# A graph layer on one core: comparisons, casts and copies of VectorE in the edge blocks written as operations of two tensors

## The chip, the cores and the metric

The kernel runs on one core of a Trainium2 chip. The metric is the device time of one execution in microseconds (us); the time before is the median of three runs.

A core has five engines that work through instruction streams of their own: TensorE (PE in the profile; its weight loads are listed as PEld), VectorE (DVE), ScalarE (ACT), GpSimd (POOL) and SyncE (SP). They wait for each other through semaphores. SBUF is the on-chip memory of 128 partitions, PSUM the memory that TensorE's products land in.

## The reference

A graph with 12,500 nodes (64 features each) and 212,500 edges, which come sorted by `dst` while the sums go to `src`. With `h` the normalised nodes:

```
h   = relu(layernorm(x))
e   = silu([h[src], h[dst], weight] @ eW1 + eb1)
e   = silu(e @ eW2 + eb2)
agg = segment_sum(e, src, 12500)
out = x + silu([h, agg] @ nW1 + nb1) @ nW2 + nb2
```

The first product is split: `h[src] @ eW1[:64] + eb1` and `h[dst] @ eW1[64:128]` are made once for each node and then picked for each edge.

## The kernel before

**Prologue.** The nodes are normalised and the two products are written to tables in HBM, `tb` for destinations and later `ta` for sources, each number as a sum of three bf16 parts. The edges lie in 208 blocks of 1024. A source's id n is split into n % 100 (its bucket, one of `NB` = 100) and n // 100 (its place within the bucket, `locE`). Bucket numbers, and destinations relative to the block's first one, go to HBM as bf16 rows (`rows`).

**Stage one, for each block: sort the edges into buckets.** The 208 blocks form 11 chunks, the first of 8 blocks and the others of 20. For a block:

- `load` (L372) fetches, from SP's queue, the block's two bf16 rows broadcast to the partitions (`bc`), a window of 112 rows of `tb` (`win`), and three rows of the weights into the tail of `pick`.
- `count` (L389) runs on VectorE. L395 makes the one-hot matrix `pick` (112 x 1024, bf16): destination number equal to the partition's number. L397 makes `oh` (100 x 1024, fp16): bucket equal to the partition's number. L400 is a scan along the edges that counts how many edges of the bucket have come so far; it starts from `carry`, the count at the end of the block before. L406 copies the last count to a small fp32 tile `end`, which becomes `carry`. L408 multiplies counts by `oh`, so that each edge keeps only the count in its own bucket.
- `send` (L417) has TensorE sum the columns of that product (`rank`, L427), which gives each edge's rank in its bucket, and multiply `pick` by `win` (L435), which gives each edge its destination's row. ScalarE copies these rows to `qs` (L442). VectorE turns rank and bucket into row addresses `to` (L445) and writes the edge's place within its bucket into the last 16 columns of `qs` (L449). GpSimd then scatters 128 rows at a time to HBM by an indirect DMA (L454), 8 scatters a block, 1661 in all. There are 8 buffers `qs` of four scatters each, and 4 of `to`.

**Stage two, for each chunk: work off the buckets.** A chunk's rows in HBM are read in 25 batches of four buckets (`fetch`, L489), five batches ahead. A batch of a chunk can be fetched only when every scatter of the chunk has landed. For 512 edges, a step, the work is: TensorE spreads the places (`s_lr`, L515), VectorE compares them with the partition number (`s_one_t`, L526, from PSUM), TensorE adds the source's row (`s_pt`), ScalarE applies silu, TensorE multiplies by `eW2` (`s_p2`), ScalarE applies silu, VectorE makes a one-hot matrix of places (`s_one`, L553: both inputs in SBUF, fp32), TensorE sums by it (`s_seg`, L587), and after each batch VectorE adds to the totals (`s_add`, L598). The last chunk's batches also produce the output.

**The order.** PE, DVE, ACT and SP run in an order written out by hand: `turn` (L605) lists the parts of a step, and at each `None` in it the loop inserts pieces of stage one for the next chunk, paced so that a chunk's sends are issued shortly before its first batch is fetched. A piece of `count` and a piece of `send` for the block before go together. GpSimd has only the scatters in its queue.

Of the kernel before, what the change touches and what calls it, by code (L numbers as in the profile page):

```python
# [28 lines left out]
F32 = mybir.dt.float32  # L29
F16 = mybir.dt.float16  # L30
BF16 = mybir.dt.bfloat16
I32 = mybir.dt.int32
AF = mybir.ActivationFunctionType
OP = mybir.AluOpType
# [4 lines left out]
P = 128  # L39
L = 125  # L40
WL = 112
BLK = 1024
# [3 lines left out]
W = 144  # L46
# [11 lines left out]
def tile_gnn(ctx: ExitStack, tc: tile.TileContext, x, src, dst, ew, eW1, eb1, eW2, eb2, nW1, nb1, nW2, nb2, out):  # L58
    nc = tc.nc
    N, D = x.shape  # L60
    H = eW2.shape[0]
    E = src.shape[0]
    assert D == 64 and H == P and N % L == 0
    NB = N // L
# [6 lines left out]
    const = ctx.enter_context(tc.tile_pool(name="const", bufs=1))  # L71
# [12 lines left out]
    zeros = const.tile([P, 4 * W], F32, name="zeros")  # L84
# [54 lines left out]
    part = const.tile([P, 1], F32, name="part")  # L139
    nc.vector.tensor_copy(part, part_i)  # L140
    part1 = const.tile([P, 1], F32, name="part1")
    nc.vector.tensor_scalar(part1, part, 1.0, None, op0=OP.add)
    nodes_i = const.tile([P, L], I32, name="nodes_i")
    nc.gpsimd.iota(nodes_i, pattern=[[1, L]], base=1, channel_multiplier=0)
    nodes1 = const.tile([P, L], F32, name="nodes1")
# [50 lines left out]
    locE = const.tile([P, 2 * TB, NP], F32, name="locE")  # L196
# [4 lines left out]
    with tc.tile_pool(name="pro", bufs=1) as pro, tc.tile_pool(name="norm", bufs=2) as np_, tc.tile_pool(  # L201
        name="nab", bufs=2
# [154 lines left out]
    with tc.tile_pool(name="ld", bufs=4) as ld, tc.tile_pool(name="ld2", bufs=NQ) as ld2, tc.tile_pool(  # L357
        name="wk", bufs=2
    ) as wk, tc.tile_pool(name="qs", bufs=8) as qsp, tc.tile_pool(name="to", bufs=4) as top, tc.tile_pool(
        name="mm", bufs=4, space=PSUM  # L360
# [7 lines left out]
        blk = {}  # L368
# [20 lines left out]
        def count(s):  # L389

            if s >= nblocks:
                return
            c = chunk_of[s]
            bc, win, pick = blk[s]
            nc.vector.tensor_scalar(pick[:WL, :], bc[:WL, 0, :], part[:WL, :], None, op0=OP.is_equal)  # L395
            oh = wk.tile([NB, BLK], F16, name="oh")
            nc.vector.tensor_scalar(oh, bc[:NB, 1, :], part[:NB, :], None, op0=OP.is_equal)  # L397
            yield
            run = wk.tile([NB, BLK], F16, name="run")
            nc.vector.tensor_tensor_scan(  # L400
                run, oh, nil.to_broadcast([NB, BLK]), carry.get(c, 0.0), op0=OP.add, op1=OP.add
            )
            yield
            end = wk.tile([NB, 1], F32, name="end")
            n = min(BLK, E - s * BLK)
            nc.vector.tensor_copy(end, run[:, n - 1 : n])  # L406
            carry[c] = end
            nc.vector.tensor_tensor(run, run, oh, op=OP.mult)  # L408
            blk[s].append(run)
            if s + 1 == nblocks or chunk_of[s + 1] != c:  # L410
                u = wk.tile([NB, 1], F32, name="u")
                for limit, op in ((chunks[c][2] * P, OP.is_gt), (chunks[c][3], OP.is_lt)):
                    nc.vector.tensor_scalar(u, end, float(limit), None, op0=op)
                    nc.vector.tensor_tensor(bad[:NB, 1:2], bad[:NB, 1:2], u, op=OP.add)
            yield

        def send(s):  # L417

            p, g = s // 2, s % 2
            c = chunk_of[s]  # L420
            _, _, cap, _, q = chunks[c]
            _, win, pick, run = blk.pop(s)
            n = min(BLK, E - s * BLK)
            nt = -(-n // P)
            rank = misc[:, (s % 2) * TB : (s % 2 + 1) * TB]
            for t in range(nt):
                nc.tensor.matmul(rank[:, t : t + 1], run[:, t * P : (t + 1) * P], ones16[:NB, :], start=True, stop=True)  # L427
            yield
            for t0 in range(0, nt, G):
                qs = qsp.tile([P, G, W], F32, name="qs")  # L430
                qp = mm.tile([P, G, H], F32, name="qp", tag="mm")
                m = min(G, nt - t0)
                for t in range(m):
                    for i in range(3):
                        nc.tensor.matmul(  # L435
                            qp[:, t, :],
                            pick[: WL + 3, (t0 + t) * P : (t0 + t + 1) * P],
                            win[: WL + 3, i, :],
                            start=i == 0,
                            stop=i == 2,  # L440
                        )
                nc.scalar.copy(qs[:, :m, :H], qp[:, :m, :])  # L442
                if t0 == 0:
                    to = top.tile([P, TB], I32, name="to")
                    nc.vector.scalar_tensor_tensor(  # L445
                        to[:, :nt], rank[:, :nt], float(cap * P + 1), bkE[:, g * TB : g * TB + nt, p], op0=OP.min, op1=OP.add
                    )
                at = g * TB + t0
                nc.vector.tensor_copy(  # L449
                    qs[:, :m, H:], locE[:, at : at + m, p][:, :, None].to_broadcast([P, m, W - H])  # L450
                )
                for t in range(t0, t0 + m):
                    k = min(P, n - t * P)
                    i = nc.gpsimd.indirect_dma_start(  # L454
                        out=q[:],
                        out_offset=bass.IndirectOffsetOnAxis(ap=to[:k, t : t + 1], axis=0),
                        in_=qs[:k, t - t0, :],
                        in_offset=None,
                    )

                    tc.declare_no_dep(i.ins, group=f"rows{c}", reason="each edge has a row of its own")
                    tc.add_to_no_dep_group(f"rows{c}", i.ins)
                yield

        def send_all(c):

            mine = [s for s in range(nblocks) if chunk_of[s] == c]
            zeros_left = list(fill(c + 1, nc.scalar, 25)) if c + 1 < len(chunks) else []
            each = -(-len(zeros_left) // len(mine))
            for s in mine:  # L470
                load(s + 2, 1)
                for f in zeros_left[:each]:
                    f()
                del zeros_left[:each]

                for i, _ in enumerate(itertools.zip_longest(count(s + 1), send(s))):
                    pending[c] -= i == PIECES - 1
                    yield
# [159 lines left out]
        for _ in count(0):  # L638
            pass
# [17 lines left out]
        at = done = 0  # L657
# [25 lines left out]
    with tc.tile_pool(name="fl", bufs=1) as fl, tc.tile_pool(name="flp", bufs=1, space=PSUM) as flp:  # L683
        fp = flp.tile([1, P], F32, name="fp")
        s = fl.tile([P, 1], F32, name="s")
        nc.vector.tensor_tensor(s, bad[:, 0:1], bad[:, 1:2], op=OP.add)
        nc.tensor.transpose(fp, s, ident)
        m = fl.tile([1, 1], F32, name="m")
# [134 lines left out]
```

## Time and profile before

| | |
|---|---|
| Median of 3 runs | 2708.69 us (2707.8 to 2714.96) |
| Profiled execution, its own time | 2708.9 us |
| Its span | 2706.9 us |
| PE busy | 2321.1 us (86%) |
| VectorE busy | 1846.2 us (68%) |
| ScalarE busy | 1204.1 us (44%) |
| GpSimd (POOL) busy | 1723.0 us (64%) |
| Scatters L454 | 1661, mean 1030 ns, 1710.3 us |
| Mean granted clock of TensorE | 0.915 |

The span is the time between the first and the last instruction that the profile shows. A row of a group names line, engine, operation, output and inputs, shapes and count, then busy time in us, the mean of one in ns, and the idle time of the engine just ahead of these instructions, with what ended it. "issue" stands for a wait that nothing in the profile explains. A row of the timeline has start and duration in us and, in brackets, the engine's idle time before it and what ended it. The slices divide the span in 40 equal parts, one digit each, in tenths of busy time.

### The profile page before, as it was taken

Reading aid. Unit: us, or ns where it says so; the run is one execution under the profiler, and the core shown is the slowest. Engines: PE = TensorE matmul, PEld = TensorE weight load, DVE = VectorE, ACT = ScalarE, POOL = GpSimd, SP = SyncE. Lnnn points to the kernel's source line nnn. Section 1 sums busy time; section 2 is a strip of 40 time slices with the busy share of each in tenths; the row PEclk is TensorE's granted clock in tenths of the full one; section 3 lists DMA queues with packets and bytes.
Section 4 is the critical chain, followed back from the end, with each engine's and each line's share of the span. In section 5 each row is a group of like instructions: output and inputs, shape, how many; then the busy total and the mean of one; then the engine's idle time right before and its main releaser. Section 6 shows DMA issues by size and latency. Waiting matters only on the chain. (4 is left out here: it accounts for less than half of the span.)

```text
span 2706.9 us, 61144 instructions
## 1 busy us (share of the span) xinstructions
PE 2321.1 (86%) x23583; PEld 2168.2 (80%) x23583; DVE 1846.2 (68%) x3287; ACT 1204.1 (44%) x2247; POOL 1723.0 (64%) x1691
## 2 busy tenths in 40 slices
PE   1656688799799699799979979979979979979998
PEld 0445577799699699799879979979979979978886
DVE  5745468688588588678768768868858868743332
ACT  2522234355355355355445435535535545534442
POOL 1036577777777777777777777777777777750000
PEclk9755689899899899999989989989989989989998
DMA  6477867987787697697797787788688758644441
GB/s 180 170 210 208 246 226 227 284 276 231 237 280 244 211 288 247 200 312 245 214 293 254 224 274 252 246 247 269 229 248 272 244 185 267 216 173 127 137 128 33
DMA packets 388692, 612.85 MB, mean 226 GB/s; under 512 B 47232, under 2 KB 294401, under 8 KB 387877
## 3 DMA queue, kind: packets, MB, share of 16 engines
q1 hardware_dynamic: 269560, 423.47, 48.7%
q0 software_dynamic: 53760, 122.94, 13.3%
q10 hardware_dynamic: 65074, 62.46, 9.4%
q8 instruction: 188, 3.08, 0.5%
q14 instruction: 110, 0.90, 0.1%
HBM read 393.49 MB, written 215.18 MB: 225 GB/s over the span
## 5 line engine op out<-in xcount | busy, mean ns | idle before, releaser
L454 POOL DMA_INDIRECT q<-qs,to x1661 | 1710.3, 1030 | 679.2 <-issue 386.4
L546 ACT ACTIVATE e<-pt 128x512 f32<-128x512 f32 x525 | 313.7, 597 | 926.5 <-PE pt L542 765.1
L573 PE MATMUL p<-w,e 128*128 128x128 f32 x4200 | 578.7, 282 | 102.3 <-ACT p L567 102.3
L573 PEld LDWEIGHTS p<-w,e 128*128 128x128 f32 x4200 | 523.6, 196 | 117.1 <-ACT p L567 104.3
L526 DVE TENSOR_SCALAR oneT<-lr,part 125x512 bf16<-125x512 f32 x525 | 392.3, 747 | 325.8 <-PE lr L521 325.7
L587 PE MATMUL seg<-one,e 128*128 128x125 f32 x4200 | 581.2, 282 | 19.8 <-DVE aggT L598 14.6
L587 PEld LDWEIGHTS seg<-one,e 128*128 128x128 f32 x4200 | 523.6, 196 | 22.6 <-ACT qs L442 11.7
L400 DVE TENSOR_TENSOR_SCAN run<-oh,end,misc 100x1024 f16<-100x1024 f16 x197 | 461.1, 2340 | 6.4 <-PE misc L427 5.8
L542 PE MATMUL pt<-oneT,a 125*128 125x256 bf16 (+1 forms) x3300 | 440.1, 272 | 0.0
L435 PE MATMUL qp<-win,pick 115*128 115x128 bf16 x4983 | 369.1, 227 | 37.1 <-DVE oneT L526 30.4
L442 ACT COPY qs<-qp 128x512 f32<-128x512 f32 x416 | 243.3, 585 | 286.5 <-PE qp L435 218.3
L435 PEld LDWEIGHTS <-pick 115*128 115x128 bf16 x4983 | 330.4, 102 | 45.3 <-issue 40.8
L553 DVE TENSOR_TENSOR one<-nodes,qt 128x500 f32<-128x500 f32 x525 | 352.2, 671 | 0.7 <-PE seg L587 0.5
L542 PEld LDWEIGHTS <-a 125*128 125x128 bf16 x3300 | 317.8, 99 | 33.5
L535 PE MATMUL pt<-ident,qt 128*128 128x128 f32 x2100 | 329.5, 281 | 3.1 <-DVE prest L187 2.2
L577 ACT ACTIVATE e<-p 128x512 f32<-128x512 f32 x525 | 313.2, 597 | 12.9 <-PE p L573 9.6
L567 ACT COPY p<-b2f 128x512 f32<-128x512 f32 x525 | 311.8, 594 | 0.0
L598 DVE TENSOR_TENSOR aggT<-aggT,seg 128x500 f32<-128x500 f32 x250 | 168.2, 673 | 152.5 <-PE seg L587 152.3
L521 PE MATMUL lr<-identb,qt 128*125 128x128 bf16 x2100 | 210.6, 224 | 62.2 <-DMA qt<-q 62.2
L521 PEld LDWEIGHTS <-qt 128*125 128x125 bf16 x2100 | 187.2, 140 | 64.0 <-DMA qt<-q 63.3
L535 PEld LDWEIGHTS pt<-ident,qt 128*128 128x128 f32 x2100 | 227.6, 144 | 4.0 <-DVE prest L187 2.3
L408 DVE TENSOR_TENSOR run<-run,oh 100x1024 f16<-100x1024 f16 x208 | 144.3, 694 | 7.1
(118 smaller groups left out, 1264.4 us busy)
## 6 DMA issues: line engine op xcount, KB each, us to landing
qt<-q SPq DMA_DIRECT2D x250, 576.0 KB
a<-ta SPq DMA_DIRECT2D x275, 384.0 KB
bc<-rows SPq DMA_DIRECT2D x208, 448.0 KB
q<-zeros ACTq DMA_DIRECT2D x40, 1462.5 KB
q<-qs,to POOLq DMA_INDIRECT x1661
win<-tb SPq DMA_DIRECT2D x208, 84.0 KB
tb<-parts SPq DMA_DIRECT2D x25, 384.0 KB
ta<-parts SPq DMA_DIRECT2D x25, 384.0 KB
```

What stands on the lines that cost most here:

```text
L400: nc.vector.tensor_tensor_scan(run, oh, nil.to_broadcast([NB, BLK]), carry.get(c, 0.0), op0=OP.add, op1=OP.add)
L435: nc.tensor.matmul(qp[:, t, :], pick[: WL + 3, (t0 + t) * P : (t0 + t + 1) * P], win[: WL + 3, i, :], start=i == 0, stop=i == 2,)
L454: i = nc.gpsimd.indirect_dma_start(out=q[:], out_offset=bass.IndirectOffsetOnAxis(ap=to[:k, t : t + 1], axis=0), in_=qs[:k, t - t0, :], in ...
L521: nc.tensor.matmul(lr[:L, t, :], loc[:, at : at + 1].to_broadcast([P, L]), identb, start=True, stop=True)
L526: nc.vector.tensor_scalar(oneT, st[k].pop("lr")[:L], part1[:L, :], None, op0=OP.is_equal)
L535: nc.tensor.matmul(pt[:, t, :], qt[:, j, :H], ident, is_transpose=True, start=t == 0, stop=False, skip_group_check=True)
L542: nc.tensor.matmul(pt[:, cols, :], a3[:L, b, i, :], oneT[:, cols, :], start=False, stop=i == 2, skip_group_check=True)
L546: nc.scalar.activation(e1, pt, AF.Silu)
L553: nc.vector.tensor_tensor(one, nodes1[:, None, :].to_broadcast([P, G, L]), qt[:, j : j + G, H : H + 1].to_broadcast([P, G, L]), op=OP.is_e ...
L573: nc.tensor.matmul(p2[:, t, :], e1[:, t, :], w2, start=False, stop=t == G - 1, skip_group_check=True)
L577: nc.scalar.activation(e2, p2, AF.Silu)
L587: nc.tensor.matmul(item[2][:, b, :], e2[:, t, :], one[:, t, :], start=j % n == 0, stop=j % n == n - 1)
```

## The change

The two comparisons in `count` took `part`, the partition's number, as a scalar for each partition. A bf16 tile `partb` with the same number in all 1024 columns is made once in the prologue, and the comparisons become operations of two tensors, `bc` and `partb`. The copy of the last count is dropped: the next scan starts from the last column of the scan's own output, an fp16 column. The multiplication writes into `oh` instead of `run`, so `run` keeps the counts and `oh` goes to TensorE. The write of the 16 columns of `qs` becomes the sum of the place and a tile of zeros. What is computed stays the same.

```diff
+    partb = const.tile([P, BLK], BF16, name="partb")
+    nc.vector.tensor_copy(partb, part.to_broadcast([P, BLK]))
...
-            nc.vector.tensor_scalar(pick[:WL, :], bc[:WL, 0, :], part[:WL, :], None, op0=OP.is_equal)
+            nc.vector.tensor_tensor(pick[:WL, :], bc[:WL, 0, :], partb[:WL, :], op=OP.is_equal)
             oh = wk.tile([NB, BLK], F16, name="oh")
-            nc.vector.tensor_scalar(oh, bc[:NB, 1, :], part[:NB, :], None, op0=OP.is_equal)
+            nc.vector.tensor_tensor(oh, bc[:NB, 1, :], partb[:NB, :], op=OP.is_equal)
             yield
             run = wk.tile([NB, BLK], F16, name="run")
             nc.vector.tensor_tensor_scan(
                 run, oh, nil.to_broadcast([NB, BLK]), carry.get(c, 0.0), op0=OP.add, op1=OP.add
             )
             yield
-            end = wk.tile([NB, 1], F32, name="end")
             n = min(BLK, E - s * BLK)
-            nc.vector.tensor_copy(end, run[:, n - 1 : n])
+            end = run[:, n - 1 : n]
             carry[c] = end
-            nc.vector.tensor_tensor(run, run, oh, op=OP.mult)
-            blk[s].append(run)
+            nc.vector.tensor_tensor(oh, run, oh, op=OP.mult)
+            blk[s].append(oh)
...
-                nc.vector.tensor_copy(
-                    qs[:, :m, H:], locE[:, at : at + m, p][:, :, None].to_broadcast([P, m, W - H])
+                nc.vector.tensor_tensor(
+                    qs[:, :m, H:],
+                    locE[:, at : at + m, p][:, :, None].to_broadcast([P, m, W - H]),
+                    zeros[:, : m * (W - H)].rearrange("p (m w) -> p m w", m=m),
+                    op=OP.add,
                 )
```

Lines move by 2 to 4 behind these edits: in the changed kernel the comparisons are L397 and L399, the scan L402, the multiplication L409, the column write L450, the scatter L458, oneT L530 and one L557.

## The prediction

> **What bounds the kernel now.** The page comes first: shares of busy time, then the slices.
>
> ```profile
> PE 2321.1 (86%) x23583; PEld 2168.2 (80%) x23583; DVE 1846.2 (68%) x3287; ACT 1204.1 (44%) x2247; POOL 1723.0 (64%) x1691
> ...
> PE   1656688799799699799979979979979979979998
> POOL 1036577777777777777777777777777777750000
> ```
>
> TensorE looks like the bound, but it dips to 7 in every third slice (67.7 us each), and a chunk of 20 blocks takes about 214 us. POOL is flat at 7, which is what an engine looks like that is fed without a break and pays something between its instructions. Next, what POOL waits for:
>
> ```profile
> POOL q L454 <- issue: 386.4, 1267, 0.4
> POOL q L454 <- ACT qs L442: 154.8, 18, 143.2
> ```
>
> 1267 of its 1661 scatters wait for "issue", 0.3 us each: nothing else was missing. One wait of 143.2 us is the prologue. From 502 us to the last scatter, which ends at 2418.46, POOL's timeline has gaps of 0.30 us and only two others, of 0.49 and 0.39. I also set each 16th scatter's start against the end of the copy (L442) and of the column write (L449) that fill its rows: from the third chunk on its rows had been ready for 9.1 us at least, up to 29 us. So POOL's queue sets the pace, and TensorE meets it at each chunk's edge, where a batch may be fetched only when all scatters of its chunk are done:
>
> ```profile
> 1580.61 0.60 ACT L546 ACTIVATE e<-pt 128x512 f32<-128x512 f32 x1 [20.76 <-DMA qt<-q]
> ```
>
> Between edges TensorE and VectorE run ahead of POOL (windows table: 1591 to 1731 us, PE 140.0 of 140 us busy, VectorE 120.6, 15 scans), a block in 9.3 us where POOL needs 8 scatters x 1.335 = 10.7. The time is therefore the head (to 330 us), plus POOL's scatters, plus 289 us of tail after 2418, when TensorE works off the last chunk. What costs POOL more than its undisturbed 0.97 + 0.30? The two timelines, POOL's and VectorE's, side by side:
>
> ```profile
> 1501.16 0.75 DVE L526 TENSOR_SCALAR oneT<-lr,part 125x512 bf16<-125x512 f32 x1
> 1501.24 0.97 POOL L454 DMA_INDIRECT q<-qs,to  x1 [0.30 <-DVE qs L449]
> ...
> 1506.02 0.67 DVE L553 TENSOR_TENSOR one<-nodes,qt 128x500 f32<-128x500 f32 x1
> 1506.33 1.28 POOL L454 DMA_INDIRECT q<-qs,to  x1 [0.30 <-DMA q<-qs,to]
> ...
> 1515.50 0.47 DVE L397 TENSOR_SCALAR oh<-bc,part 100x1024 f16<-100x1024 bf16 x1
> 1515.65 1.16 POOL L454 DMA_INDIRECT q<-qs,to  x1 [0.31 <-DMA q<-qs,to]
> ```
>
> A scatter that starts under a comparison from PSUM (L526) takes 0.97. One that starts under L553, a tensor_tensor with both inputs in SBUF, takes 0.31 longer, and under L397, a tensor_scalar from SBUF, 0.19 longer. I did this for all scatters between 500 and 2417 us (1437, in all 89.7 us over 0.967 each). Running at the scatter's start, with the number of scatters and their total excess: L553, 236, 64.2 us; L408, 58, 13.3 us; L397, 30, 5.9 us; L395, 27, 4.9 us. All others (scan L400, L526, L598, nothing) come to under 2 us in over 1,000 scatters. The excess is the VectorE instruction's end less the scatter's start less about 0.12 us. So one rule explains 98% of it: a scatter does not begin until the VectorE instruction under way is done, if that has two SBUF inputs or is one of the fast tensor_scalars.
>
> **The Trainium skill.** "SBUF — State Buffer", section "Who interferes with whom": VectorE and GpSimd share a port pair; a VectorE instruction in a two-port mode, or with two SBUF inputs while GpSimd reads SBUF, makes the later one wait to the end. The trace agrees (0.95 of starts under L553 are held). The same section infers that tensor_tensor leaves descriptor generation alone; L408, the same kind as the new comparisons, held 90% of the scatters that began under it, so the measurement decides. "VectorE: DVE Perf Modes", section "The perf-mode tier table": 16-bit tensor_scalar in SBUF reaches 4x, tensor_tensor 2x. The trace agrees for 1024 elements:
>
> ```profile
> L408 DVE TENSOR_TENSOR run<-run,oh 100x1024 f16<-100x1024 f16 x208 | 144.3, 694 | 7.1
> L397 DVE TENSOR_SCALAR oh<-bc,part 100x1024 f16<-100x1024 bf16 x208 | 101.8, 489 | 3.0 <-DMA tb<-parts 3.0
> L395 DVE TENSOR_SCALAR pick<-bc,part 112x1024 bf16<-112x1024 bf16 x208 | 100.6, 483 | 6.2 <-DMA bc<-rows 6.2
> L449 DVE COPY qs<-locE 128x64 f32<-128x64 f32 x415 | 83.7, 202 | 0.2 <-ACT e L546 0.2
> L406 DVE CAST end<-run 100x1 f32<-100x1 f16 x208 | 30.8, 148 | 0.0
> L414 DVE TENSOR_TENSOR bad<-bad,u 100x1 f32<-100x1 f32 x22 | 3.5, 161 | 0.8
> ```
>
> **The change, part by part.** The orders of PE, ACT, POOL and SP stay as they are; on VectorE 207 casts go and one instruction is added in the prologue.
>
> *The two comparisons.* They take L408's 0.694 us in place of 0.483 and 0.489: both are 16-bit throughout, 1024 long. That is +0.42 us of VectorE a block. What counts is how often they hold a scatter. A scatter starts every 1.335 us, 0.749 per us. An instruction of length T holds those that start in its first T - 0.12 us, by half of that on average. For 0.694: 0.749 x 0.574² / 2 = 0.123 us a block. For 0.483 and 0.489: 0.049 + 0.051 = 0.100 together. Measured (180 blocks): L408 0.074, L395 and L397 0.060 together, each 0.60 of that count. A reason: pick and oh follow L553 directly, and a scatter that L553 held starts its successor 1.27 us later, past their end. With the same 0.60 the new pair costs 2 x 0.074 = 0.148, so +0.088 a block. Laid out from the three starts themselves (L553 at 0, pick at 0.59, oh at 1.19 instead of 0.98, one scatter start in each 1.27 us; releases at 0.57, 0.95, 1.34 become 0.57, 1.16, 1.76), the group's mean delay goes from (0.57 x 0.285 + 0.38 x 0.19 + 0.32 x 0.23) / 1.27 = 0.24 to (0.57 x 0.285 + 0.59 x 0.297 + 0.11 x 0.55) / 1.27 = 0.31, +0.07. Without any such shelter it is 0.246 - 0.060 = +0.186. Some 200 of the 208 blocks lie where POOL is fed: +14, +18, +37 us. I take +16, near the first two, since the shelter is in the measurement. A gain is not excluded: a shift of phase moves starts among L553, L408 and the pair; I allow -10 us for it.
>
> *The column write* (L449) becomes tensor_tensor: 0.161 + 63 elements x 1.03 ns (slope between L187's 256 elements in 420 ns and L553's 500 in 671) = 0.226, +0.02 us. As a holder of scatters: 0.749 x 0.106² / 2 x 2 = 0.008 us a block against 0.005 now: +1 us at most. I take +1, from 0 to 2.
>
> *The cast and the carry.* VectorE saves 0.148, about 0.18 between starts, and the multiplication comes that much earlier. The cast, one element, held nothing. More instructions (oneT 135 for 58, one 145 for 60) now wait for an earlier VectorE instruction, which before had the cast's wait ahead of them: 162 x about 0.1 us (L408 behind its wait starts 0.03 after the cast's end where others start 0.08 before) = 16 us over the run.
>
> *VectorE's own time*: +0.42 + 0.05 - 0.18 + 0.08 = +0.37 us a block. Cover: VectorE stood idle 19.4 us in the 15 blocks of the window above, 1.3 us a block, and rows lie ready 9 us ahead of POOL. If that were gone it would cost 208 x 0.37 = 77 us. It is missing only in the head, around the first scatter (172 us) and from 260 to 350 us where POOL waited for rows: about 7 blocks, +2 us (0 to 5).
>
> *oh in place of run.* The multiplication writes into oh, so TensorE's rank matmuls hold oh instead of run; there are two of each, and the next oh that reuses the buffer comes two blocks later, behind them: nothing. *partb*: one write of 1024 elements, between 0.6 and 1.2 us, inside VectorE's 15.9 us wait for the first ids: nothing.
>
> Sum: 16 + 1 + 2 = +19 us on the profiled execution's 2708.9 (span 2706.9, 2 us around it), which is 0.2 from the median: **2728 us**.
>
> **Rivals.** *Only the two-port modes hold POOL, or POOL profits more than it loses* (7%): then L395's and L397's 10.8 us in 180 blocks go, 12.5 us over all, less the head's 2: 2698. It speaks for it that these are held scatters now; against it that L408 holds as many as any. It decides once fewer than 4 in 10 of the starts under the new comparisons are held: 0.4 x 0.148 is today's 0.060. *The phases fall so that the delay hardly rises* (17%): pick held scatters that L408 or L553 would otherwise have held. Today L408 and the pair are at 0.60 of chance and L553 above it, so such shifts are of the size of the effect; about 2713. *The comparisons run at one element a cycle* (4%): 0.671 + 524 x 1.03 ns = 1.21 us each, 0.749 x 1.09² / 2 = 0.445 a block each, less shelter +0.47 to +0.83 a block: some 2840, with VectorE's +1.46 above its idle 1.3. L408's length speaks against it.
>
> **How the numbers follow.** 72% for my forecast, whose own range is 2717 to 2748 (full chance rate +37 and +3); the rest as above. Under 0.3% (8 us) this kernel's time can't be told from no change. Faster 0.07, same 0.17, slower 0.76. The range 2709 to 2748 leaves out the first and the last rival and little else.
>
> **What would show it.** Both comparisons at about 0.69; POOL's scatters from 1.030 to about 1.040 on average, still 0.30 apart; scatters that start under them longer than 0.97; the last scatter ending near 2437 and the tail unchanged at 289; VectorE busy near 1910. I am wrong if starts under them take 0.97, if POOL waits for rows past 530 us, or if the chunk's edge no longer waits for scatters.

## The result, and the profile after

The changed kernel takes 2823.19 us (median of 6 runs, 2810.6 to 2839.7) where the kernel before takes 2708.26 on the same chip: 1.0431 times as long, with an interval of 1.0389 to 1.0473. The forecast was 2728, with 2748 as its upper end: the direction was right, the size was not. The profiled execution took 2839.7 us, with a span of 2837.9, 131.0 more than before.

On some chips the kernel before took 3,300 us and more, and in the traces of its variants taken there TensorE stops hundreds of times for "issue" (in `cmp_only`, below, 774 times and 470 us in all; once and 0.2 us in the kernel before as profiled above) and POOL has gaps of several us; what ran there is marked *(stalled chip)* below, and of it only the lengths of the scatters are used, not the time.

The page of the changed kernel, its first lines and the slices:

```profile
span 2837.9 us, 61053 instructions
...
PE 2357.0 (83%) x23583; PEld 2193.3 (77%) x23583; DVE 1909.3 (67%) x3080; ACT 1204.8 (42%) x2247; POOL 1856.5 (65%) x1691
...
PE   1665787798798699699889879969879979979998
POOL 1046677777777777777777777777778777770000
```

TensorE, ScalarE and VectorE are busy about as forecast (VectorE 1909.3 against some 1910). POOL has 133.5 us more to do, 1856.5 against 1723.0, and the span is 131.0 longer. Its main wait (us in all, times, the longest) and its row in the groups:

```profile
POOL q L458 <- issue: 410.2, 1339, 2.2
```

```profile
L458 POOL DMA_INDIRECT q<-qs,to x1661 | 1843.9, 1110 | 674.8 <-issue 410.2
```

It waits as before, 0.30 us between two scatters and nothing else; from the 224th scatter on, the gaps add up to 433.7 us, before to 433.2. It was not starved. Each scatter is longer: 1.110 us on average in place of 1.030. The chunk's edge still waits for the last rows, as it did (20.76 us before):

```profile
1657.03 0.60 ACT L550 ACTIVATE e<-pt 128x512 f32<-128x512 f32 x1 [20.51 <-DMA qt<-q]
```

The groups of the changed VectorE instructions, each shape apart:

```profile
L397 DVE TENSOR_TENSOR pick<-bc,partb 112x1024 bf16<-112x1024 bf16 x208 | 143.0, 687 | 6.4 <-DMA bc<-rows 6.4
L399 DVE TENSOR_TENSOR oh<-bc,partb 100x1024 f16<-100x1024 bf16 x208 | 142.7, 686 | 2.5 <-DMA tb<-parts 2.5
L450 DVE TENSOR_TENSOR qs<-locE,zeros 128x64 f32<-128x64 f32 x415 | 90.8, 219 | 0.2 <-issue 0.2
```

The forecast had 0.694, 0.694 and 0.226; 0.687, 0.686 and 0.219 came. No instruction is slow. The 131.0 us are laid out in time like this: the 224th scatter starts at 508.12 instead of 500.99 (+7.1), the last one ends at 2548.75 instead of 2418.46 (+130.3), and the tail behind it is 289.2 us instead of 288.4. What grew lies between the 224th scatter and the last, and it is the time by which scatters exceed 0.967 us: 212.3 us in place of 89.7, +122.7. Below, this time is called the excess; a scatter with an excess was held, and it was released at its start plus its excess.

The two timelines side by side, VectorE's and POOL's, show which scatters these are:

```profile
1498.99 0.69 DVE L409 TENSOR_TENSOR oh<-run,oh 100x1024 f16<-100x1024 f16 x1
1499.14 1.50 POOL L458 DMA_INDIRECT q<-qs,to  x1 [0.30 <-issue]
1499.59 0.22 DVE L450 TENSOR_TENSOR qs<-locE,zeros 128x64 f32<-128x64 f32 x1
1499.73 0.67 DVE L602 TENSOR_TENSOR aggT<-aggT,seg 128x500 f32<-128x500 f32 x1
1500.31 0.74 DVE L530 TENSOR_SCALAR oneT<-lr,part 125x512 bf16<-125x512 f32 x1
1500.95 2.73 POOL L458 DMA_INDIRECT q<-qs,to  x1 [0.30 <-issue]
1500.97 0.67 DVE L557 TENSOR_TENSOR one<-nodes,qt 128x500 f32<-128x500 f32 x1
1501.56 0.69 DVE L397 TENSOR_TENSOR pick<-bc,partb 112x1024 bf16<-112x1024 bf16 x1
1502.16 0.69 DVE L399 TENSOR_TENSOR oh<-bc,partb 100x1024 f16<-100x1024 bf16 x1
...
1511.43 0.67 DVE L557 TENSOR_TENSOR one<-nodes,qt 128x500 f32<-128x500 f32 x1
1511.68 1.27 POOL L458 DMA_INDIRECT q<-qs,to  x1 [0.30 <-issue]
```

The scatter at 1499.14 starts under the multiplication, which ends at 1499.68. It is 0.53 too long, so it was released at 1499.67. A hold by the multiplication alone would have ended 0.12 to 0.14 before its end, at some 1499.55; 1499.67 is 0.14 before the end of the column write behind it (1499.81). The next one, at 1500.95, starts 0.02 before L557 and is held through L557, L397 and L399: 1.76 too long, released at 1502.71 where L399 ends at 1502.85. The last one, at 1511.68, starts 0.25 into L557 and is released at the end of L557, as the prediction had it, although the same two comparisons follow.

Joined for all scatters of both kernels from 500 us on, by the VectorE instructions through which each was held:

| held through | before: scatters, us | after: scatters, us |
|---|---|---|
| one alone | 224, 64.1 | 129, 40.8 |
| multiplication alone | 52, 13.3 | none |
| pick or oh alone | 51, 10.0 | 35, 8.2 |
| multiplication and column write | none | 82, 38.0 |
| pick and oh | none | 38, 37.4 |
| one, pick and oh | none | 34, 60.0 |
| one, multiplication and column write | none | 14, 16.8 |
| others | few, 2.3 | few, 11.2 |

Four lines that did not exist before hold 152 us. The holds by a single instruction went down, from 87 to 49. 77 scatters are held for more than 0.7 us; before, there was one.

How far a scatter is held depends on when it starts. All 108 that were held under the multiplication with the write behind it went at the end of the write or later, wherever in the multiplication they started (those that start when the write already overlaps it stand under "others" in the table). For the comparisons it is otherwise: 38 scatters start 0.01 to 0.03 us ahead of the start of pick (L397), and 24 of them were held to the end of oh, 14 not at all; the 28 that start 0.03 to 0.50 into pick all went at its end; of 18 that start 0.50 to 0.53 into it, 14 were held to the end of oh.

### The profile page after: what moved, and what is told of

It reads as the page before. It is cut to its first block, busy times and chain, and to the rows that moved or that the text cites. A ratio compares the mean times of both kernels' runs of the same rounds, so it can differ in the third digit from the quotient of the medians.

```text
span 2837.9 us, 61053 instructions
## 1 busy us (share of the span) xinstructions
PE 2357.0 (83%) x23583; PEld 2193.3 (77%) x23583; DVE 1909.3 (67%) x3080; ACT 1204.8 (42%) x2247; POOL 1856.5 (65%) x1691
## 4 chain that ended last, share of the span: by engine, by line
PE 46%; POOL 13%; DMA 12%; issue 12%; DVE 7%; ACT 1%; SPq 0%; DVEq 0%; ACTq 0%; POOLq 0%
POOL q L458 13%; PE seg L591 11%; PE p L577 10%; DMA q<-qs,to 10%; PE pt L546 7%; PE qp L436 5%; PE pt L539 5%; DVE run L402 3%; PE lr L525 3%; PE z L344 1%; PE z L343 1%; PE o L350 1%; DVE one L557 1%; DVE oneT L530 1%; PE misc L428 1%
## 5 line engine op out<-in xcount | busy, mean ns | idle before, releaser
L458 POOL DMA_INDIRECT q<-qs,to x1661 | 1843.9, 1110 | 674.8 <-issue 410.2
L577 PE MATMUL p<-w,e 128*128 128x128 f32 x4200 | 585.8, 284 | 106.8 <-ACT p L571 106.8
L591 PE MATMUL seg<-one,e 128*128 128x125 f32 x4200 | 591.0, 285 | 78.9 <-DVE aggT L602 73.8
L577 PEld LDWEIGHTS p<-w,e 128*128 128x128 f32 x4200 | 531.6, 198 | 122.3 <-ACT p L571 108.9
L591 PEld LDWEIGHTS seg<-one,e 128*128 128x128 f32 x4200 | 530.3, 198 | 87.3 <-ACT e L581 55.3
L530 DVE TENSOR_SCALAR oneT<-lr,part 125x512 bf16<-125x512 f32 x525 | 392.1, 747 | 293.7 <-PE lr L525 292.2
L402 DVE TENSOR_TENSOR_SCAN run<-oh,run,misc 100x1024 f16<-100x1024 f16 x197 | 461.1, 2341 | 5.3 <-PE misc L428 4.6
L546 PE MATMUL pt<-oneT,a 125*128 125x256 bf16 (+1 forms) x3300 | 446.2, 274 | 0.0
L557 DVE TENSOR_TENSOR one<-nodes,qt 128x500 f32<-128x500 f32 x525 | 352.6, 672 | 0.5 <-PE seg L591 0.5
L546 PEld LDWEIGHTS <-a 125*128 125x128 bf16 x3300 | 320.1, 100 | 36.1
L581 ACT ACTIVATE e<-p 128x512 f32<-128x512 f32 x525 | 314.1, 598 | 16.6 <-PE p L577 13.3
L602 DVE TENSOR_TENSOR aggT<-aggT,seg 128x500 f32<-128x500 f32 x250 | 167.9, 672 | 112.1 <-PE seg L591 110.2
L446 DVE SCALAR_TENSOR_TENSOR to<-misc,bkE 128x8 int32<-128x8 f32 x208 | 31.6, 152 | 240.3 <-issue 140.1
```

The costliest lines, as they stand in the source:

```text
L402: nc.vector.tensor_tensor_scan(run, oh, nil.to_broadcast([NB, BLK]), carry.get(c, 0.0), op0=OP.add, op1=OP.add)
L458: i = nc.gpsimd.indirect_dma_start(out=q[:], out_offset=bass.IndirectOffsetOnAxis(ap=to[:k, t : t + 1], axis=0), in_=qs[:k, t - t0, :], in ...
L530: nc.vector.tensor_scalar(oneT, st[k].pop("lr")[:L], part1[:L, :], None, op0=OP.is_equal)
L546: nc.tensor.matmul(pt[:, cols, :], a3[:L, b, i, :], oneT[:, cols, :], start=False, stop=i == 2, skip_group_check=True)
L557: nc.vector.tensor_tensor(one, nodes1[:, None, :].to_broadcast([P, G, L]), qt[:, j : j + G, H : H + 1].to_broadcast([P, G, L]), op=OP.is_e ...
L577: nc.tensor.matmul(p2[:, t, :], e1[:, t, :], w2, start=False, stop=t == G - 1, skip_group_check=True)
```

## The experiments

The theory: where one VectorE instruction with two SBUF inputs follows another without a break, a scatter can be held to the end of the whole run of them and not only of the one under way. The first rival: the comparisons and the write each hold as forecast, and the time went elsewhere (the starting column of the scan, or rows that come late). The second: the two-input kind as such is what costs, run or no run.

**Break the runs.** The changed kernel with a memset of one column ahead of each comparison and each column write, 832 more VectorE instructions of 0.059 us. It was first run on a stalled chip (`gaps`), then on an undisturbed one (`gaps_again`).

```diff
+            nc.vector.memset(gap[:, 0:1], 0.0)
             nc.vector.tensor_tensor(pick[:WL, :], bc[:WL, 0, :], partb[:WL, :], op=OP.is_equal)
             oh = wk.tile([NB, BLK], F16, name="oh")
+            nc.vector.memset(gap[:, 1:2], 0.0)
             nc.vector.tensor_tensor(oh, bc[:NB, 1, :], partb[:NB, :], op=OP.is_equal)
...
+                nc.vector.memset(gap[:, 2:3], 0.0)
                 nc.vector.tensor_tensor(
                     qs[:, :m, H:],
```

> The changed kernel with a memset of one column of SBUF (about 0.06 us) ahead of pick, of oh and of each column write, which adds some 830 instructions to VectorE. Theory of runs: the short instruction that reads nothing lets a waiting scatter in, no scatter above 1.7 us except behind L561 and L412 that still touch, 2720 to 2745 us although VectorE has about 50 us more to do. Rival (the loss comes from VectorE's longer work, its added waits, or from holds to each instruction's own end that merely fall at its start): no gain, 2815 us or more.

> The changed kernel with a one-column memset ahead of pick, oh and each column write, once more because the first chip was disturbed. Theory of runs: ratio to the kernel before 1.005 to 1.015, no scatter above 1.7 us. Rival (VectorE's longer work or added waits): 1.04 or more.

`gaps` (stalled chip) had scatters of 1.034 us on average and one held for more than 0.7 us. `gaps_again` took 2727.13 us (2722.45 to 2729.99) against 2708.51 before, 1.0066 times (1.0048 to 1.0084). Its scatters, and from its timelines a scatter under L561, the "one" of this kernel, with the multiplication and then memset and write behind it:

```profile
L462 POOL DMA_INDIRECT q<-qs,to x1661 | 1725.3, 1039 | 683.7 <-issue 410.6
```

```profile
1418.05 0.67 DVE L561 TENSOR_TENSOR one<-nodes,qt 128x500 f32<-128x500 f32 x1
1418.12 1.45 POOL L462 DMA_INDIRECT q<-qs,to  x1 [0.30 <-issue]
1418.63 0.69 DVE L412 TENSOR_TENSOR oh<-run,oh 100x1024 f16<-100x1024 f16 x1
```

1.039 us a scatter in place of 1.110. The excess from 500 us on is 105.3, which is 15.6 over before, and three scatters are held for more than 0.7. The scatter shown starts 0.07 into L561 and goes at that instruction's end, 0.48 late; of the 20 scatters of the changed kernel that start 0.07 to 0.09 into a "one" with multiplication and write behind it, 14 are held to the end of the write, 1.20 on average, and 6 to the end of the "one". More VectorE work, and 96 us less: instructions that touch cost it. The comparisons and the write with two inputs are all still there, which the second rival can't account for. And the first can't either: the scan's column is there too. For the pair it can be seen directly: the scatters held under the multiplication (84) now go at its own end. For the comparisons it can't, as only five scatters start within 0.06 us of a "one" ahead of them (none is held, but in the changed kernel 47 do); whether the memset ends such holds or moves the starts away from them, this run doesn't separate. What is left of excess is close to what the prediction had summed for the whole, 16 + 1, with a last scatter at 2438.84 where it said "near 2437". That is in part luck: the comparisons come to 15.5 us in place of 10.8, the multiplication to 32.8 in place of 13.3, and the "one" to 55.5 in place of 64.3, where the sum had the increase in the comparisons.

**Take one input out of SBUF.** The node numbers that L553 compares with are copied to PSUM, so that it has one input in SBUF; once in the kernel before (`before_psum`), once in the changed one (`after_psum`).

```diff
-        misc = sgp.tile([P, 4 * TB], F32, name="misc")
+        misc = sgp.tile([P, 4 * TB + L], F32, name="misc")
+        nodesP = misc[:, 4 * TB :]
+        nc.vector.tensor_copy(nodesP, nodes1)
...
-                nodes1[:, None, :].to_broadcast([P, G, L]),
+                nodesP[:, None, :].to_broadcast([P, G, L]),
```

> The kernel before with the node numbers that L553 compares kept in PSUM, so that this instruction has one input in SBUF and lasts as long. If two SBUF inputs are what holds a scatter: no scatter starting under it is held, its 64 us of excess (74 over the whole run) go, 2635 to 2655 us, and POOL stays the bound. If any long VectorE instruction on SBUF holds: no change, 2700 to 2717 us.

> The changed kernel with the same move of the node numbers to PSUM. Theory of runs: the run L557, pick, oh shrinks to pick, oh (1.2 us at most) and L557's own holds go; what is left is the pair and the multiplication with the column write: 2680 to 2730 us, no scatter above 2.3 us. If VectorE's work or waits were the cause: 2800 us or more.

The group of the scatters, of `before_psum` and of `after_psum`:

```profile
L456 POOL DMA_INDIRECT q<-qs,to x1661 | 1647.6, 992 | 688.0 <-issue 384.0
```

```profile
L460 POOL DMA_INDIRECT q<-qs,to x1661 | 1715.9, 1033 | 677.6 <-issue 411.0
```

`before_psum`: 2655.24 us (2653.29 to 2665.92), 0.9812 times before (0.9785 to 0.9838). The excess falls from 89.7 to 36.1: under L553 (there L555), which still takes 0.67 us, 1.0 us is left of 64. So it is the second SBUF input that holds, and this kernel beats both. The scatters' own time falls by 62.7 us and the span by 52.7: POOL's gaps grow by 8.6 us.

`after_psum`: 2711.75 us (2707.8 to 2721.79), 1.0014 times (1.0004 to 1.0023). With L557 out of the runs their excess is 91.9: multiplication and column write 80 times, 41.4 us; oh alone 88 times, 31.9; pick and oh 7 times, 6.9; and some 44 scatters start within 0.06 us of the start of a "one" that pick follows, each at 0.97. The same edit is worth 111 us here and 53 before.

**The holds by themselves.** Two kernels that leave the layer out: scatters one after the other on POOL, and on VectorE groups of instructions set apart by comparisons from PSUM of changing length, so that the phase drifts.

```diff
+        def narrowing():
+            one()
+            nc.vector.tensor_tensor(c16[1][:112], a16[:112], b16[:112], op=OP.is_equal)
+            nc.vector.tensor_tensor(c16[2][:100], a16[:100], b16[:100], op=OP.is_equal)
+
+        def widening_flat():
+            mult100()
+            colflat()
...
+            for k in range(40):
+                kind()
+                filler(128 + 9 * k)
+                filler(330)
```

> Not the graph layer: it copies x to the output and leaves all else out. POOL issues 560 scatters back to back while VectorE runs seven stretches: one tensor_tensor (1024 bf16, both inputs in SBUF) between fillers that read PSUM; two in a row; three in a row; a fp32 one of 500 followed by two; the same followed by two tensor_scalars; the same with a one-column memset between the three; one followed by a fp32 one of 64. Theory of runs: excess over 0.97 us up to 0.6 in the first stretch, 1.2 in the second, 1.8 in the third and fourth, 0.6 in the fifth and sixth, and in the seventh always to the end of the short one. Theory of single instructions: nowhere above 0.6.

> Not the graph layer: it copies x to the output and leaves all else out. POOL issues 860 scatters back to back while VectorE repeats seven groups 40 times each, with fillers of varied length so that scatters arrive at all phases, also at the first instruction's start: one fp32 tensor_tensor of 500 and two of 1024 16-bit, all on 128 partitions; the same on 128, 112 and 100; a multiplication on 100 followed by a flat write of 64 on 128; the same with the strided column write of the kernel; the strided write behind a multiplication on 128; the first with two tensor_scalars behind it; the second with memsets between. If arrival at the start makes the run hold as one: excess of about 1.7 us in the first two groups, none above 0.7 in the last two. If it is the width or the pattern of the second instruction: the hold goes to the end of the column write in the groups where it is wider than the one before, or strided.

`bench` (773.67 us, all instructions on 128 partitions) was a miss for the theory in its plain form: two or three two-input instructions of 1024 elements in a row held scatters for 0.43 us at most, all released when the instruction under which they started ended. But in these groups the scatters came 0.11 to 0.50 into an instruction, never at its start. `bench2` (1232.45 us, stalled chip) varied the partitions. One on 100 partitions with one on 128 behind it, and three in a row on 128:

```profile
233.45 0.68 DVE L106 TENSOR_TENSOR c<-a,c 100x1024 f16<-100x1024 f16 x1
233.49 1.61 POOL L81 DMA_INDIRECT q<-qs,to  x1 [0.30 <-issue]
234.05 0.22 DVE L117 TENSOR_TENSOR c<-a,b 128x64 f32<-128x64 f32 x1
...
42.01 0.67 DVE L103 TENSOR_TENSOR c<-a,b 128x500 f32<-128x500 f32 x1
42.32 1.19 POOL L81 DMA_INDIRECT q<-qs,to  x1 [0.30 <-issue]
42.60 0.69 DVE L123 TENSOR_TENSOR c<-a,b 128x1024 bf16<-128x1024 bf16 x1
```

The first scatter goes 0.68 after the start of L106, 0.14 before the end of L117, its follower; so did each that was held under that group (38 of 38, up to 0.64 late), and each that was held where the write was strided like the layer's (36 of 36). The second goes 0.53 after the start of L103, at its end less 0.14; so did each of 39. With the first instruction on 128 partitions the strided write did not prolong the hold (0.54 to 0.55 after the start). Two things differ there, 100 partitions or 128 and fp16 or bf16; the pattern of the write is not what does it. Groups on 128, 112 and 100 partitions, in that order like L557, L397 and L399, were released at the end of the first for each start from 0.05 to 0.42 into it. A start within 0.03 of the first one's start did not occur in these, so the long holds of the layer were not reproduced alone. In the group of two with a short write behind (`bench`) it occurred four times, and none of the four was held.

**Each edit alone.** From the kernel before: the comparisons alone (`cmp_only`), the column write alone (`col_only`), the carry with the multiplication into oh alone (`carry_only`); from the changed kernel: the column write back to the copy (`after_col_back`), or the memset ahead of the column write only (`gap_col`). All of them came on stalled chips, also in repeats.

`cmp_only`, and the same for pick; `col_only`, with `after_col_back` as its reverse; `carry_only`; `gap_col`, each cut to its core:

```diff
-            nc.vector.tensor_scalar(oh, bc[:NB, 1, :], part[:NB, :], None, op0=OP.is_equal)
+            nc.vector.tensor_tensor(oh, bc[:NB, 1, :], partb[:NB, :], op=OP.is_equal)
...
-                nc.vector.tensor_copy(
+                nc.vector.tensor_tensor(
...
-            nc.vector.tensor_copy(end, run[:, n - 1 : n])
+            end = run[:, n - 1 : n]
...
+                nc.vector.memset(gap[:, 2:3], 0.0)
```

> Only the two comparisons become tensor_tensor; the cast, the column write and the multiplication stay as before. Theory of runs (a scatter that arrives as a run of two-input instructions begins is held to the end of the run L553, pick, oh): scatters of about 2.7 and 2.1 us appear, the comparisons account for roughly half of the loss, 2760 to 2785 us. Theory of the prediction (each instruction holds only to its own end): no scatter above 1.7 us, 2718 to 2730 us.

> Only the column write of qs becomes tensor_tensor. Theory of runs: the multiplication and the column write behind it hold as one, so scatters that start under the multiplication are held about 0.13 us longer than its end, and L553 followed by both can hold 1.2 us; 2725 to 2755 us. Theory of the prediction (single instructions): at most +1 us, 2706 to 2712 us.

> Only the carry changes: no cast, the next scan starts from the last fp16 count, the product goes into oh. Both theories: no new two-input instruction, so within 8 us of the kernel before, 2700 to 2717 us. If L553 and the multiplication, which now can follow each other without the cast between them, form a run, scatters up to 2.2 us appear and it costs 10 to 20 us: 2718 to 2730 us.

> Only the two comparisons become tensor_tensor, on an undisturbed chip. Theory of runs with the phases set by the column write: without the multiplication and column write holding as one, few scatters arrive at the start of L553, so hardly any is held through all three: 2720 to 2750 us. If the run forms by itself: 2760 to 2785 us. Theory of the prediction: 2718 to 2730 us.

> Only the column write becomes tensor_tensor, on an undisturbed chip. Theory of runs: scatters under the multiplication are held to the end of the column write, 40 us of excess more: 2735 to 2760 us. Theory of the prediction: 2706 to 2712 us.

> Only the cast is dropped and the product goes into oh, on an undisturbed chip. No new two-input instruction, but the multiplication now follows L553 directly: 2700 to 2722 us. If waits or the carry itself cost something: more.

> Only the two comparisons become tensor_tensor, cast kept. As cmp_only_2: 2720 to 2750 us if long holds need the column write, 2760 us or more if the comparisons make them alone.

> Only the column write becomes tensor_tensor. As col_only_2: 2735 to 2760 us if the multiplication and the column write hold as one, 2706 to 2712 us by the prediction.

> The changed kernel with a one-column memset only ahead of each column write. If the multiplication and the column write holding as one is the root (it also sets the phase in which scatters arrive at the start of L557): 2725 to 2750 us and few scatters above 1.7 us. If the run of L557, pick, oh forms by itself: holds of 2.1 and 2.7 us stay, 2770 to 2800 us.

> The changed kernel with the column write back as a copy. If the column write is the root: 2720 to 2750 us, no hold to the end of the column write, few scatters above 1.7 us. If the comparisons are: 2770 us or more, with scatters of 2.1 and 2.7 us.

> The kernel before with the two comparisons alone changed. Theory: the holds seen in this kernel elsewhere add 27 to 31 us to those of before, so 2735 to 2740 us, between 2728 and 2750, and no hold through L553 and both comparisons; the two single edits then add up to about 75 of the 115 us, and the remainder of some 40 us belongs to the two together. Rival (the comparisons alone bring the long holds, and the column write only adds its pairs): about 2708 + 65 = 2773 us.

> The kernel before with the column write alone changed to the sum with zeros. Theory (runs of two-input instructions hold a scatter through): where POOL sets the pace, the pairs of multiplication and column write cost 48 to 54 us in holds against 13 before, so about 2708 + 48 = 2756 us, between 2740 and 2765, with no long holds through three instructions. Rival (the cost arises only where comparisons and column write are both changed, because then the phases lock): within 8 us of before.

| run | us, before beside it | excess of some 1,465 scatters, us | kinds that matter here |
|---|---|---|---|
| `cmp_only` | 3395.43, 3410.75 | 117.8 | one 54.1; multiplication 42.3 |
| `cmp_only_2` | 3308.64, 3330.29 | 120.7 | one 54.3; multiplication 44.7 |
| `cmp_only_3` | 3326.18, 3332.81 | 120.5 | one 53.7; multiplication 46.9 |
| `cmp_only_4` | 3397.64, 3404.35 | 119.9 | one 52.4; multiplication 47.0 |
| `col_only` | 3369.2, 3410.75 | 141.1 | multiplication and write 54.1 (98 times) |
| `col_only_2` | 3311.21, 3330.29 | 137.7 | multiplication and write 48.3 (88) |
| `col_only_3` | 3305.22, 3332.81 | 138.2 | multiplication and write 54.4 (99) |
| `col_only_4` | 3367.63, 3404.35 | 143.0 | multiplication and write 54.1 (95) |
| `carry_only` | 3458.44, 3410.75 | 83.9 | multiplication 32.6 |
| `carry_only_2` | 3351.08, 3330.29 | 85.6 | one 41.8; multiplication 26.0 |
| `gap_col` | 3364.22, 3332.81 | 102.1 | one 53.2; multiplication 28.7 |
| `after_col_back` | 3355.15, 3332.81 | 103.8 | one 46.6; multiplication 29.6 |

Here POOL has up to several us between two scatters, and longer scatters show no cost in the time: `col_only_4` has 53 us more of excess than the kernel before had in its own profile, on another chip, and its time is 0.9887 of before's (0.9822 to 0.9951). Therefore the times that these expectations name were not tested, and why single edits come out a per cent faster or slower on such chips stays open. What they show is which holds occur. In `col_only_4`, and for comparison a scatter of the kernel before under the same multiplication with a copy behind it:

```profile
719.17 0.69 DVE L408 TENSOR_TENSOR run<-run,oh 100x1024 f16<-100x1024 f16 x1
719.24 1.61 POOL L457 DMA_INDIRECT q<-qs,to  x1 [3.87 <-ACT e L580]
719.78 0.22 DVE L449 TENSOR_TENSOR qs<-locE,zeros 128x64 f32<-128x64 f32 x1
```

```profile
659.33 0.69 DVE L408 TENSOR_TENSOR run<-run,oh 100x1024 f16<-100x1024 f16 x1
659.45 1.41 POOL L454 DMA_INDIRECT q<-qs,to  x1 [0.30 <-DVE end L406]
659.94 0.19 DVE L449 COPY qs<-locE 128x64 f32<-128x64 f32 x1
```

The upper one goes at 719.88, with the write's end (720.00); the lower one at 659.89, with the multiplication's (660.02), while the copy still runs. So the column write's new form alone makes the pair, in all four repeats. The comparisons alone never brought a hold through one, pick and oh: 58 scatters started within 0.06 us of the start of such a "one" in the four runs, and none was held beyond it. But the changed kernel has 42 of its 47 such starts, and all 34 long holds among them, within 0.005 to 0.025 us ahead of the "one", and only 8 of the 58 fall there (5 held to its end, 3 not at all). So the rival that the comparisons alone bring the long holds is not borne out here, on few cases, and where POOL sets the pace it was not tested. With the comparisons and the column write as a copy (`after_col_back`) there were 6 holds over 0.7, most of them through pick and oh, one (1.76) through the "one" (there L554) as well, so a long hold can come without the new column write; with both, and only the pair of multiplication and write broken (`gap_col`), none. The changed kernel as it is was not run on a stalled chip, so the count of 77 has no direct counterpart there.

**Why they come together.** I followed the 72 holds of the changed kernel through pick and oh, with or without L557 ahead, one scatter back. In 58 of them the scatter before had been released at the end of a column write. It then takes 0.967 and POOL 0.30 to the next start. VectorE meanwhile has, behind that write, L602, L530 and then L557 (34 times; in one of them L600 for L602), or L530, L557 and then L397 (24 times). Both are fixed chains: in the lines above L450 ends at 1499.81, and L557 starts at 1500.97, 0.02 after the scatter. So a hold by the write sets POOL to VectorE's own rhythm, and the next scatter falls on the first instruction of the next run. 47 of 179 starts of a "one" that pick follows have a scatter start within 0.06 us, against 2 in the kernel before and 5 in `gaps_again`; of the 47, 34 were held through all three, and the others to the end of L557 or not at all. `after_psum` has some 44 such starts and no cost from them. This chain is read from the one trace of the changed kernel; no run set the phase by itself.

## Why the prediction was wrong, point by point

- *POOL's queue sets the pace; head, scatters, tail.* Right. +7.1 in the head (2 forecast), +122.7 in holds, +0.5 in gaps, +0.7 in the tail make the 131.0. "Tail unchanged at 289": 289.2.
- *The comparisons take 0.694.* Right, 0.687 and 0.686. VectorE's longer work stayed covered: the gaps of POOL did not grow. `after_psum` has as much work on VectorE (1908.2 us) and stands at 1.0014.
- *A scatter does not begin until the VectorE instruction under way is done, if that has two SBUF inputs.* Right for what it was drawn from; the cause is confirmed by moving one input to PSUM. The Trainium skill, "SBUF — State Buffer", section "Who interferes with whom", which lets the later access wait to the end of such an instruction, describes what is seen; its inference that tensor_tensor leaves descriptor generation alone can't be carried over to a whole scatter (64 us of holds that went with the second SBUF input). Whether a held scatter waits to read its addresses `to` or to generate descriptors, no run separates.
- *"releases at 0.57, 0.95, 1.34 become 0.57, 1.16, 1.76".* This is the step that failed. It lets a held scatter go at the end of each instruction, also where another of the kind follows at once. The kernel before had no such case to read it from: behind L408 came a copy, behind L553 the cast, a tensor_scalar or the scan, behind L395 a tensor_scalar; and only 2 scatters started within 0.06 us of an L553 that L395 follows. I carried the rule over to a sequence, and to starts, that no line showed. Of the 45 scatters that started within 0.03 us of the run's start, 34 were released at 1.75, behind all three. The sum also took the starts as even over 1.27 us, and they were not: 47 lay within 0.06 us of the start of such a run, where even spacing gives some 16 (estimate: 174 runs x 0.12 us x 0.749 per us). With the runs broken (`gaps_again`) 15.6 us came for this step and the write together where 17 were forecast, but only 4.7 of them under the comparisons.
- *The column write, "+1 us at most".* The term most wrong in size. It was priced by its own 0.106 us of holding, but it is what stands behind the multiplication: 13.3 us of holds by the multiplication became 54.8 by multiplication and write, with or without L557 ahead. And it put the scatters on the starts of the next run, where holds through both comparisons, with or without L557, come to 97.4 us.
- *"The cast, one element, held nothing."* True of the cast itself. But it stood between L553 and L408, 174 times; without it L557, L409 and L450 follow each other at once, and 14 scatters were held through these three, 16.8 us. In the four `col_only` runs, where the cast stands, no scatter was.
- *"With the same 0.60 the new pair costs 2 x 0.074".* The shelter did not stay. The phases did move, as the second rival had it, but to the other side: it rested on scatters that L553 releases, which start past the comparisons; those that the write releases start on them.
- *Rivals.* Only the two-port modes hold: refuted by the prediction's own test, since all 46 scatters that started 0.03 to 0.53 us into a pick were held. Favourable phases: refuted. One element a cycle: refuted by 0.687. The range had none of the interplay in it, since every case in it priced each instruction alone.

Open: why a scatter that comes at the start of L557 mostly waits for all three, while one that comes 0.25 later goes at L557's end, and why such starts end in two ways (34 of 45 at L557, 24 of 38 at pick were held to the end of oh); why a run from 100 to 128 partitions holds through whenever the scatter comes; and how the +115 us divides between the two edits where POOL sets the pace, since their single times were taken where it doesn't.

## What to carry to other kernels

Where GpSimd feeds indirect DMAs without a break, look not only at how long a VectorE instruction with two SBUF inputs is, but at what follows it: a second one at once can make the pair hold the queue as one, and a short instruction that reads nothing between them (0.06 us here) gave back 96 us of 115. Better still, put one of the two inputs into PSUM: one tile moved made the kernel before 1.9% faster. A cost rule read from a trace holds for the neighbourhoods that the trace has; where an edit makes a new one, the sum needs a bound for that.

## What the runs showed of the hardware

- A scatter of 128 rows takes 0.967 us on GpSimd and 0.30 passes to the next; a VectorE instruction with two SBUF inputs under which it starts puts it off to that instruction's end less 0.12 to 0.14 us; L553 with one input in PSUM did not (1.0 us in all in place of 64).
- Two of them in a row, fp16 on 100 partitions and then fp32 on 128, put each scatter that they held off to the end of the second (all 108 in the changed kernel; up to 0.64 us in `bench2`); on 128 and 128 only to the end of the first (up to 0.51).
- Three in a row (128, 112 and 100 partitions) held a scatter for 1.76 us where it started within 0.03 us of the first one's start, in 34 of 45 cases; the last two of them held it for 1.18 us where it started 0.01 to 0.03 us ahead of theirs, in 24 of 38, and not at all in the other 14.
- Where POOL had gaps of several us, a kernel with 143 us of held scatters was no slower than the one before beside it (0.9887, `col_only_4`).
